# Causal row maxima in a four-block kernel: a fused masked reduction on VectorE against a split over three engines

## The chip, the cores and the metric

The kernel runs on one core of a Trainium2 chip. The metric is device time in microseconds (us), the median of several executions. Engines go by the profile's short names: PE (TensorE, matmuls and transposes), DVE (VectorE), ACT (ScalarE), POOL (GpSimd), SP (SyncE, which issues most DMAs). SBUF is the on-chip memory; PSUM is the small memory that matmuls write, eight banks of 512 fp32 numbers per partition.

## The reference, cut to what matters

Four blocks run one after the other on x of shape (2, 1024, 128), each followed by a layer norm: a retention block, then block 2 (causal attention with 16 heads of width 8, and four experts), then a block of attention over the full row, then a matmul with ternary weights. The change lies in the causal attention of the second block:

```python
scores = jnp.einsum('bhqd,bhkd->bhqk', q, k) / np.sqrt(HEAD_DIM)
causal = jnp.tril(jnp.ones((t, t), dtype=bool))
scores = jnp.where(causal, scores, -jnp.inf)
attn = jax.nn.softmax(scores, axis=-1)
out = jnp.einsum('bhqk,bhkd->bhqd', attn, v)
```

The softmax subtracts the largest score of each row, so each query needs the maximum over the keys that it may see.

## The kernel before, in words

**Stages.** The retention block fills the first 255 us or so. From there on, one hand-written schedule of 224 ticks (`chain_tick`, run from tick 3 on by the loop at L1102, ticks 0 to 2 by hand before it) does both attentions; the experts, projections and norms of the blocks are cut into pieces that `side_work` puts ahead of the ticks by due times. All of it is in manual order: each engine runs its instructions in the order in which the Python code issues them.

**Steps and items.** A step (L307) is one attention (a = 0 causal, a = 1 full), one sequence b, one block k of 512 queries, one group g of four heads. Its score items (`s_items`, L313 to L319) are tiles of 128 queries (number c) by up to 512 keys. In a causal step with k = 0 there are four, the **diagonal items**, c = 3, 2, 1, 0, with n = 512, 384, 256, 128 keys; the last 128 keys of each are the ones that the mask cuts. A causal step with k = 1 has four full items (512 keys of the first half) and after them its four diagonal items. So the causal attention has 96 items, ticks 0 to 95, of which 64 are diagonal; the full attention has ticks 96 to 223, eight items of 512 keys a step.

**A tick** does five things. `score` (L324) computes the item's scores by queries, one PSUM bank a head (tile `sc`). `maxima` (L338) reduces each to row maxima (`parts`): a diagonal tile by the fused `tensor_tensor_reduce` with the tile `causal` on DVE (L345; the profile shows a custom instruction and an accumulator read), another by `tensor_reduce` (L350). `shifted` (L373) computes the scores of the item 11 ticks back again, transposed, keys by queries (`sct`), now with the maxima subtracted, which enter as a row of `qT`; `exps` (L390) takes the exponential on ACT (L394), `bar` (L396) zeroes the masked corner on POOL (L402), and one tick later `product` (L408) multiplies with the values (tile `acc`), ACT copies the result out (L416, L419) and POOL adds it up (L420). Heads go in two halves: scores of heads 0 and 1 with transposed scores of 2 and 3, then the other way round. PE's order in a tick is thus sc0 sc1 sct2 sct3 sc2 sc3 sct0 sct1 acc, ACT's is e2 e3 e0 e1 (exponentials), then the copy of acc.

**From maxima to qT.** When a step's last item is through, `shifts` (L352) reduces `parts` to one number per query and head (tile `lowered`), `enter` (L362), one tick later, transposes it on PE (`m_ps`), ACT copies it (L370), and a DMA on SP's queue (L371) puts it into `qT`. The step's first transposed item is read 11 ticks after its first score item (AHEAD = 11).

**The ring.** All of these PSUM tiles, and those of the side work, take turns in a ring of eight banks (`ring_of`, L161). A tick takes nine, so `acc` takes the bank of the same tick's sc0 and cannot start before DVE is done with it; the next tick's tiles follow in the same way.

**Side work that the prediction names.** In ticks 3 and 4 `padding` for the second sequence (L230) fills tiles on POOL (L232 to L235) and `kT` on ACT (L236). In ticks 7 to 25 `mla_inputs` (L250) makes the second sequence's queries and keys; its rotary step works on POOL (L266, L269). From about tick 36 the experts take two tiles of the ring a tick: `ph` (L940, biased and rectified by ACT at L945 and DVE at L943) or `pmoe` (added up by DVE at L955).

## Time and profile before

| what | value |
|---|---|
| median of 4 runs (range) | 1208.35 us (1208.13 to 1210.31) |
| the profiled execution's own time | 1206.45 us |
| its span, first to last instruction | 1204.7 us |
| ticks 0 to about 17 (260 to 330 us) | PE 63.24 of 70.00 us busy, DVE 49.31, ACT 28.16, POOL 27.02 |
| the rest of the causal ticks (330 to 655 us) | PE 308.07 of 325.00 us busy, DVE 221.58, ACT 191.04, POOL 136.93 |
| most of the full attention (655 to 1150 us) | PE 469.77 of 495.00 us busy, DVE 385.19, ACT 343.27, POOL 173.62 |

An engine is busy while it runs an instruction. Matmul ends are modelled, so a busy PE need not be at its peak. A line such as "L345 DVE CUSTOM ... xN | busy, mean" is a group of like instructions; what follows the second bar is the engine's idle time ahead of them and what ended it. In the timeline a row gives start, length, engine, line, tiles and how many were merged, and in brackets the idle time ahead of it with the engine and tile that ended it.

### The profile page before, as it was taken

What the parts mean: (1) busy time and instruction counts of PE and PEld (TensorE: products, weight loads), DVE (VectorE), ACT (ScalarE), POOL (GpSimd) and SP (SyncE); (2) the same over time, 40 slices, a digit from 0 to 9 for tenths busy, and PEclk for the clock granted to TensorE, in tenths of its full rate; (3) what the DMA queues carried; (4) which work ended last, traced back from release to release, by engine and by line L of the source; (5) the groups of instructions that cost most, each with busy time, mean ns of one, the idle gap of its engine ahead of it and who ended that gap; (6) DMA issues with size and microseconds to landing.
All of it is one profiled execution on the core that took longest, in us unless ns stands there. A gap on an engine that the chain in (4) does not pass through costs nothing.

```text
span 1204.7 us, 22194 instructions
## 1 busy us (share of the span) xinstructions
PE 1111.5 (92%) x8554; PEld 607.3 (50%) x8554; DVE 830.9 (69%) x1822; ACT 711.0 (59%) x1439; POOL 478.1 (40%) x491
## 2 busy tenths in 40 slices
PE   6999999988899999999999999999989989998993
PEld 4888778755444555445544454444433333333321
DVE  3666677657667666676676667767788878888822
ACT  2455544432656645664565557555768877886892
POOL 3465544513645433452434334333233333333342
PEclk8999999965989999999999999999999999999996
DMA  8212121002000000010010001000100000000000
GB/s 263 66 45 54 36 45 41 23 11 78 19 10 10 1 1 2 4 20 1 1 19 2 1 3 19 2 1 1 19 10 2 2 2 10 1 2 10 2 1 9
DMA packets 14840, 25.56 MB, mean 21 GB/s; under 512 B 2960, under 2 KB 8400, under 8 KB 14352
## 3 DMA queue, kind: packets, MB, share of 16 engines
q1 hardware_dynamic: 14080, 22.30, 7.6%
q8 instruction: 67, 1.10, 0.4%
q0 software_dynamic: 224, 1.05, 0.2%
q10 hardware_dynamic: 432, 0.81, 0.2%
q14 instruction: 37, 0.30, 0.1%
HBM read 10.13 MB, written 1.05 MB: 9 GB/s over the span
## 4 chain that ended last, share of the span: by engine, by line
PE 73%; DVE 15%; POOL 5%; issue 3%; ACT 2%; DMA 1%; SPq 0%; POOLq 0%; DVEq 0%; ACTq 0%
PE sc L82 16%; PE acc L82 15%; PE sct L82 12%; PE pmoe L82 5%; PE ph L82 5%; DVE parts L350 4%; DVE spare L345 2%; PE pv L82 2%; PE py L82 2%; PE pr L82 2%; PE pg L82 1%; PE pout L707 1%; ACT es L394 1%; PE o_ps L186 1%; PE psc L82 1%
## 5 line engine op out<-in xcount | busy, mean ns | idle before, releaser
L394 ACT ACTIVATE es<-sct 128x512 f32<-128x512 f32 (+3 forms) x896 | 427.2, 559 | 213.5 <-PE sct L82 161.0
L350 DVE TENSOR_REDUCE parts<-sc 128x1 f32<-128x512 f32 x640 | 397.0, 682 | 94.7 <-PE sct L82 67.2
L82 PE MATMUL sc<-kT,qT 32*128 32x512 f32 (+3 forms) x1792 | 427.0, 587 | 0.9 <-DVE parts L345 0.9
L82 PE MATMUL sct<-qT,kT 32*128 32x512 f32 (+3 forms) x1792 | 411.7, 577 | 1.4 <-DMA qT<-m_rows 1.1
L420 POOL TENSOR_TENSOR oT<-oT,part 128x512 f32<-128x512 f32 (+3 forms) x192 | 217.1, 1131 | 398.9 <-ACT part L419 394.9
L82 PE MATMUL acc<-es,v_aug 128*32 128x512 f32 (+3 forms) x1792 | 222.8, 561 | 39.9 <-DVE parts L350 28.4
L82 PEld LDWEIGHTS sc<-kT,qT 32*128 32x128 f32 x1792 | 169.9, 190 | 141.0 <-DVE parts L350 74.2
L82 PEld LDWEIGHTS sct<-qT,kT 32*128 32x128 f32 x1792 | 179.2, 184 | 45.1 <-issue 22.4
L345 DVE CUSTOM_DVE_ANT_0 spare<-sc,causal 128x512 f32<-128x512 f32 (+3 forms) x256 | 125.5, 490 | 55.5 <-PE sc L82 21.3
L82 PEld LDWEIGHTS acc<-es,v_aug 128*32 128x32 f32 x1792 | 37.9, 108 | 197.1 <-DVE parts L350 112.5
L419 ACT COPY part<-acc 128x512 f32<-128x512 f32 (+3 forms) x192 | 105.8, 551 | 42.7 <-PE acc L82 34.5
L402 POOL TENSOR_SCALAR_AFFINE_SELECT es<-es 128x512 f32<-128x512 f32 x64 | 40.6, 634 | 101.6 <-ACT es L394 101.6
L764 ACT ACTIVATE og<-pt,cols_sb 128x128 f32<-128x128 f32 x128 | 46.4, 468 | 36.5 <-PE pt L756 36.5
L82 PEld LDWEIGHTS pmoe<-m_w,hT 128*128 128x128 f32 x512 | 59.6, 192 | 15.9 <-DVE parts L350 8.8
L82 PE MATMUL pmoe<-m_w,hT 128*128 128x128 f32 x512 | 65.0, 280 | 0.4
L82 PE MATMUL ph<-xnT,m_w 128*128 128x512 f32 x128 | 62.4, 610 | 0.0
L118 POOL TENSOR_TENSOR rstd<-rstd,nhalf 128x4 f32<-128x4 f32 (+1 forms) x44 | 54.6, 1242 | 3.6
L943 DVE TENSOR_SCALAR hT<-ph,cols_sb 128x512 f32<-128x512 f32 x32 | 24.0, 751 | 34.6 <-PE ph L82 34.6
L955 DVE SCALAR_TENSOR_TENSOR moe_acc<-pmoe,oh,moe_acc 128x128 f32<-128x128 f32 x64 | 22.4, 351 | 35.3 <-PE pmoe L82 34.9
L661 ACT COPY v<-pv 128x1024 f32<-128x1024 f32 x16 | 16.2, 1012 | 51.5 <-PE pv L82 51.5
L638 POOL TENSOR_TENSOR swap<-swap,r_cs 128x1024 f32<-128x1024 f32 x16 | 37.7, 2359 | 21.5 <-DMA swap<-plain 21.5
L82 PE MATMUL py<-r_wo,og 128*128 128x128 f32 x256 | 35.3, 296 | 6.2 <-DVE mrope L262 3.9
(177 smaller groups left out, 1200.0 us busy)
## 6 DMA issues: line engine op xcount, KB each, us to landing
swap<-plain SPq DMA_DIRECT2D x64, 128.0 KB
qT<-dense SPq DMA_DIRECT2D x32, 64.0 KB
kT<-dense SPq DMA_DIRECT2D x32, 64.0 KB
m_w<-in_m_w SPq DMA_DIRECT2D x2, 1024.0 KB
x<-in_x SPq DMA_DIRECT2D x4, 256.0 KB
mcs<-in_m_const SPq DMA_DIRECT2D x4, 256.0 KB
out<-ob SPq DMA_DIRECT2D x4, 256.0 KB
r_rest<-in_r_const POOLq DMA_DIRECT2D x1, 774.0 KB, 7.6
```

The source lines that it names most:

```text
L82: nc.tensor.matmul(o, lhsT, rhs, start=start, stop=stop)
L118: nc.gpsimd.tensor_tensor(r, r, nhalf[:, :n], ALU.pow)
L345: nc.vector.tensor_tensor_reduce(out=spare[:, :n], in0=sc[:, :n], in1=causal[:, BT - n :], scale=1.0, scalar=-3.0e38, op0=ALU.add, op1=ALU ...
L350: nc.vector.tensor_reduce(part, sc[:, :n], AX.X, ALU.max)
L394: nc.scalar.activation(es[n_item][:, j, :n], sct[:, :n], AF.Exp, scale=scale)
L402: nc.gpsimd.affine_select(out=d, in_=d, pattern=[[0, GH], [1, P]], compare_op=ALU.is_ge, fill=0.0, base=0, channel_multiplier=-1,)
L419: nc.scalar.copy(part[:, lo:], acc[:, lo:])
L420: nc.gpsimd.tensor_tensor(sums[i][:, lo:], sums[i][:, lo:], part[:, lo:], ALU.add)
L638: nc.gpsimd.tensor_tensor(swap[n], swap[n], table(n, 1), ALU.mult)
L764: nc.scalar.activation(og[:, a, g, :], pt[a][:, g, :], AF.Identity, bias=col("gn_b", h), scale=col("gn_w", h))
L943: nc.vector.tensor_scalar(hT[:, f, :], ph, bias, 0.0, ALU.add, ALU.max)
L955: nc.vector.scalar_tensor_tensor(acc[:, c, :], py[:, :P], oh[:, c, e : e + 1], acc[:, c, :], ALU.mult, ALU.add)
```

## The change

A diagonal tile is no longer reduced in one fused instruction. ACT copies its last 128 columns into one SBUF tile for all four heads (`corner`, two buffers); POOL overwrites the masked part there with -3e38 (`mask`, one `affine_select`); DVE takes the row maxima of all four heads at once from it (`barred`, one reduction, which stands one tick later between that tick's two halves), and, from PSUM, of the open columns ahead of the corner, n - 128 of them (none for c = 0). `parts` gets one more column; the open part of c = 0, which does not exist, is filled with -3e38 by POOL. In the steps with k = 1 the diagonal items now come first and the full items after them. In the steps with k = 0, whose last item is a diagonal one, `shifts` and `enter` come one tick later. The tile `causal` goes, with its set-up; the zeros that two DMAs took from it come from a small tile.

```diff
--- before.py
+++ after.py
@@ -3,7 +3,7 @@
 import concourse.bass as bass
 import concourse.tile as tile
 from concourse import mybir
-from concourse.masks import make_causal_mask, make_identity
+from concourse.masks import make_identity
 from concourse._compat import with_exitstack
 
 F32 = mybir.dt.float32
@@ -24,6 +24,7 @@
 NE, FF = 4, 512
 NF = FF // P
 NEG = -1.0e9
+LOWEST = -3.0e38
 NH = NG * GH
 VW = HD + 1
 VN = (NH - 1) * VW + HW
@@ -84,10 +85,8 @@
 
     ident = const.tile([P, P], F32, name="ident")
     make_identity(nc, ident)
-
-    causal = const.tile([P, BT], F32, name="causal")
-    nc.gpsimd.memset(causal, 0.0)
-    make_causal_mask(nc, causal[:, BT - P :], mask_val=-1.0e30)
+    zeros = const.tile([GH, P], F32, name="zeros")
+    nc.gpsimd.memset(zeros, 0.0)
     nhalf = const.tile([P, 16], F32, name="nhalf")
     nc.gpsimd.memset(nhalf, -0.5)
     ones = const.tile([P, P], F32, name="ones")
@@ -308,17 +307,21 @@
         (a, b, k, g) for a in range(2) for b in range(B) for k in range(NB) for g in range(NG)
     ]
 
+
     s_items, t_items = [], []
     for i, (a, b, k, g) in enumerate(steps):
         if a == 0:
+            s_items += [(i, c, k, (c + 1) * P) for c in reversed(range(NC))]
             s_items += [(i, c, half, BT) for half in range(k) for c in range(NC)]
-            s_items += [(i, c, k, (c + 1) * P) for c in reversed(range(NC))]
             t_items += [(i, kt, max(0, kt * P - k * BT)) for kt in range((k + 1) * NC)]
         else:
             s_items += [(i, c, half, BT) for half in range(NB) for c in range(NC)]
             t_items += [(i, kt, 0) for kt in range(T // P)]
     s_last = {it[0]: n for n, it in enumerate(s_items)}
+
+    s_done = {i: n + (steps[i][0] == 0 and steps[i][2] == 0) for i, n in s_last.items()}
     t_last = {it[0]: n for n, it in enumerate(t_items)}
+    corners = {}
     parts, lowered, es, sums, pools, o_tok = {}, {}, {}, {}, {}, []
 
     def score(item, heads):
@@ -326,7 +329,9 @@
         a, b, k, g = steps[i]
         tok = slice(k * BT + c * P, k * BT + (c + 1) * P)
         if i not in parts:
-            parts[i] = small.tile([P, NC, GH, NB], F32, tag="parts", name="parts")
+            parts[i] = small.tile([P, NC, GH, NB + 1], F32, tag="parts", name="parts")
+            if a == 0:
+                nc.gpsimd.memset(parts[i][:, 0, :, k : k + 1], LOWEST)
         got = []
         for j in heads:
             sc = slot("sc")
@@ -335,24 +340,46 @@
             got.append((j, sc))
         return got
 
-    def maxima(item, got):
+    def diagonal(item):
+
         i, c, half, n = item
         a, b, k, g = steps[i]
-        for j, sc in got:
-            part = parts[i][:, c, j, half : half + 1]
-            if a == 0 and half == k:
-                spare = early.tile([P, BT], F32, tag="spare", name="spare")
-                nc.vector.tensor_tensor_reduce(
-                    out=spare[:, :n], in0=sc[:, :n], in1=causal[:, BT - n :], scale=1.0,
-                    scalar=-3.0e38, op0=ALU.add, op1=ALU.max, accum_out=part,
+        return a == 0 and half == k
+
+    def maxima(item, got):
+
+        i, c, half, n = item
+        open_n = n
+        if diagonal(item):
+            open_n = n - P
+            if item not in corners:
+                corners[item] = small.tile([P, GH, P], F32, tag="corner", name="corner", bufs=2)
+            for j, sc in got:
+                nc.scalar.copy(corners[item][:, j, :], sc[:, open_n:n])
+        if open_n:
+            for j, sc in got:
+                nc.vector.tensor_reduce(
+                    parts[i][:, c, j, half : half + 1], sc[:, :open_n], AX.X, ALU.max
                 )
-            else:
-                nc.vector.tensor_reduce(part, sc[:, :n], AX.X, ALU.max)
+
+    def mask(item):
+
+        d = corners[item]
+        nc.gpsimd.affine_select(
+            out=d, in_=d, pattern=[[0, GH], [-1, P]], compare_op=ALU.is_ge, fill=LOWEST,
+            base=0, channel_multiplier=1,
+        )
+
+    def barred(item):
+        i, c, half, n = item
+        nc.vector.tensor_reduce(
+            parts[i][:, c, :, half + 1], corners.pop(item), AX.X, ALU.max
+        )
 
     def shifts(i):
 
         a, b, k, g = steps[i]
-        n_half = NB if a else k + 1
+        n_half = NB if a else k + 2
         lowered[i] = small.tile([P, GH, NC], F32, tag="lowered", name="lowered")
         nc.vector.tensor_reduce(
             lowered[i].rearrange("p j c -> p c j"), parts[i][:, :, :, :n_half], AX.X, ALU.max,
@@ -450,6 +477,8 @@
     def starts(a, b, k):
         return s_first[step_of(a, b, k, 0)]
 
+    done_at = {n: i for i, n in s_done.items()}
+
     def chain_tick(tick):
         si = tick if tick < n_items else None
         ti = tick - AHEAD if 0 <= tick - AHEAD < n_items else None
@@ -458,18 +487,21 @@
             got_t = shifted(ti, t_heads) if ti is not None else ()
             if si is not None:
                 maxima(s_items[si], got_s)
+                if s_heads[0] == 0 and 0 < si and diagonal(s_items[si - 1]):
+                    barred(s_items[si - 1])
             if ti is not None:
                 exps(ti, got_t)
         if ti is not None:
             bar(ti)
-        if si is not None and s_last[s_items[si][0]] == si:
-            shifts(s_items[si][0])
+        if si is not None and diagonal(s_items[si]):
+            mask(s_items[si])
+        if tick in done_at:
+            shifts(done_at[tick])
         ai = tick - AHEAD - 1
         if 0 <= ai < n_items:
             product(ai)
-        si = tick - 1
-        if 0 <= si < n_items and s_last[s_items[si][0]] == si:
-            enter(s_items[si][0])
+        if tick - 1 in done_at:
+            enter(done_at[tick - 1])
         ai = tick - AHEAD - 3
         if 0 <= ai < n_items and t_last[t_items[ai][0]] == ai:
             finish(t_items[ai][0])
@@ -1006,7 +1038,7 @@
             for g in range(NG):
                 nc.sync.dma_start(
                     out=qT[b][ONE::HW, g, :],
-                    in_=causal[:GH, :P].unsqueeze(1).to_broadcast([GH, T // P, P]),
+                    in_=zeros.unsqueeze(1).to_broadcast([GH, T // P, P]),
                 )
         tp = transposed(x2[b][k], "x2_ps")
         x2T = scratch("joT", "x2T", (P, BT))
```

## The prediction, on record before the changed kernel ran

> **What bounds the kernel now.** The page first: PE is the busiest engine, and the chain of waits that ended last is mostly PE. The fused maxima (spare, L345) hold 2% of the chain's span, other maxima (L350) 4%.

> ```profile
> span 1204.7 us, 22194 instructions
> PE 1111.5 (92%) x8554; PEld 607.3 (50%) x8554; DVE 830.9 (69%) x1822; ACT 711.0 (59%) x1439; POOL 478.1 (40%) x491
> ...
> PE 73%; DVE 15%; POOL 5%; issue 3%; ACT 2%; DMA 1%; SPq 0%; POOLq 0%; DVEq 0%; ACTq 0%
> ```

> So 2% of 1204.7, 24 us, is all that faster masked maxima could take directly. The windows by stage bound PE's idle time in the causal ticks at (70.00 - 63.24) + (325.00 - 308.07) = 24 us. Then the timeline, for what a tick waits for. Ticks with expert work (heavy, 4.5 to 5.3 us) differ from those without (light, 2.0 to 3.3 us). A heavy one with a full item, DVE and PE:

> ```profile
> 557.98 2.48 DVE L350 TENSOR_REDUCE parts<-sc 128x1 f32<-128x512 f32 x4 [0.30 <-PE sc L82]
> ```
> ```profile
> 556.82 0.70 PE L82 MATMUL sc<-kT,qT 32*128 32x512 f32 x2
> ...
> 558.82 0.64 PE L82 MATMUL acc<-es,v_aug 128*32 128x256 f32 x8 [0.60 <-DVE parts L350]
> ```

> The tick starts at 556.82; sc0 is ready 1.16 us later; its reduction lasts 0.68; acc starts 0.16 after that, having stood still for 0.60. The chain sc0, maximum, acc sets this tick's first part (2.00 us), since the transposed tiles are small. In a light step (487 to 498 us) DVE is the bound: fused reductions follow each other without a gap, at 0.84 us (512 columns), 0.71 (384), 0.57 (256) and 0.44 (128):

> ```profile
> 488.18 0.69 DVE L345 CUSTOM_DVE_ANT_0 spare<-sc,causal 128x512 f32<-128x512 f32 x1 [1.37 <-PE sc L82]
> ...
> 488.79 0.08 DVE L345 DVE_READ_ACCUMULATOR2_ANT parts<- 128x1 f32 x1
> 489.02 0.69 DVE L345 CUSTOM_DVE_ANT_0 spare<-sc,causal 128x512 f32<-128x512 f32 x1
> ```

> That is 4 x (0.84 + 0.71 + 0.57 + 0.44) = 10.24 us of the step's 11.0 (487.02 to 498.0).

> **Part 1: DVE's work.** Plain reductions: 0.682 us at 512 columns (L350), 0.276 at 128 (L986); by a straight line 0.41 at 256, 0.55 at 384. Four of 512 take 2.48 together, so the next starts 0.60 after the last, 0.08 less than one lasts. Per step: open parts 4 x (0.47 + 0.33 + 0.20) = 4.0; four corner reductions of 128x512 like L220 (0.679; 0.60 apart) 2.4; sum 6.4, or 7.7 if nothing overlaps. DVE saves 2.5 to 3.8 us a step, 40 to 61 us over 16 steps, worth something only where DVE is late.

> **Part 2: ACT's copies.** 256 of 128 columns. One lasts 0.291 (L419, 128x128), but four exponentials of 128 columns take 0.79, that is 0.17 apart:

> ```profile
> 558.12 0.79 ACT L394 ACTIVATE es<-sct 128x128 f32<-128x128 f32 x4 [1.37 <-PE sc L82]
> ```

> So 44 to 74 us. A light step has exponentials (2.15 + 1.64 + 1.2 + 0.9 = 5.9), copies of acc (0.62 + 0.48 + 0.37 + 0.27 = 1.7), m_rows 0.25: 7.9 us of 11.0. With 16 x 0.17 it is 10.6, with 16 x 0.29 12.5. I take 0.17, the row of the same engine, shape and direction; the other end is a rival.

> **Part 3: an order between ACT and DVE.** In the changed program every reduction of an open part waits for ACT's copy of the same bank, not for PE. So the chain becomes sc0, copy, maximum, acc: 0.29 for the copy and a handover. No handover from ACT to DVE stands alone in the trace; it lies between 0 and the 0.16 of DVE to PE; I take 0.10. The second pair is copied only after two exponentials.

> [...]

> Heavy ticks, start to acc, from the timeline (score columns, transposed columns): (512,384) 2.00 with a gap of 0.21, (512,256) 1.99 with 0.39, (512,128) 2.00 with 0.60, (512,512) 1.93 to 1.99, (384,512) 1.97, (256,512) 1.96, (128,512) 1.57, (384,256) 1.66, (256,128) 1.35. After: with sc0 ready at 1.16, 0.90 and 0.72 us, plus 0.29 + 0.10, the reduction (0.55, 0.41, 0.28) and 0.16, acc starts at 2.26, 1.86, 1.55 in the three diagonal ticks; the fourth has no reduction on DVE from PSUM, 1.57.

> **Part 4: the new order (k = 1).** The diagonal items now meet the small transposed tiles, the full items the large ones. Leading four ticks before: 2.00 + 1.99 + 2.00 + 1.99 = 7.98; after 2.26 + 1.86 + 1.55 + 1.57 = 7.24: -0.74. Trailing four before: 1.93 + 1.97 + 1.96 + 1.57 = 7.43; after 4 x 1.95 = 7.8: +0.4.

> **Part 5: POOL.** 64 masks at 0.634 (L402, same extent), 41 us, and 16 small fills (0.33 each by L233). POOL is 42% busy here, so its time is covered; if not, the mask is late, and DVE, which waits for it in the middle of the next tick, holds the reductions of heads 2 and 3 and so the ring. In a light tick the mask ends some 0.6 to 0.9 us ahead of that point (exponentials end at +3.6, two selects, 4.9; DVE is there at about +5.5). Behind the rotary pair (2.36 + 1.27 us, four times in ticks 11 to 25) it is late. Between 0 and 4 x 3.6 us; I take +1.0, because the causal zeroing (L402), which acc needs, waits behind the same pair already.

> **Part 6: the rest, at nothing.** shifts and enter a tick later in eight k = 0 steps: six ticks are left until qT is read, over 12 us, against 4.98 of the longest m_rows landing on the chain; SP's order stays as it is. The set-up of causal goes at the start, under the loads. Ticks 3 and 4: copies stand behind four fills of kT (4.27 us), a mask behind four fills of qT (3.91); DVE comes out level there, then gains.

> **The sum** (a step's eight ticks have a leading and a trailing half):
> - heavy leading halves, 3 (ticks 40, 72, 80): 3 x -0.74 = -2.2
> - heavy trailing halves, 5 (36, 44, 68, 76, 92): +2.0
> - heavy k = 0 step, 1 (48): 0.25 + 0.2 + 0.2 = +0.65
> - light k = 0 steps, 4 (12, 52, 56, 60): DVE no longer the bound; PE's own sum there is score parts 1.79 + 1.66 + 1.35 + 1.57 = 6.4, acc 1.06 + 0.85 + 0.64 + 0.43 = 3.0, transposes 0.9: 10.3; with ACT at 10.6 I take 10.6 for 11.0: -1.6
> - light leading halves, 5 (16, 24, 32, 64, 88): -0.3 each by the same relief: -1.5
> - light trailing halves, 3 (20, 28, 84): +0.2 each: +0.6
> - ticks 0 to 11, where DVE works almost without a gap: three steps save 2.5 or more each, some 7.5, but most of it is lost again behind the fills and at the side work's own chain; between -7.5 and +1 (copies that wait out the fills), I take -1.5
> - POOL +1.0

> Together -2.6 us. The profiled execution took 1206.45: 1203.85. The median lies 1.90 above that execution: 1205.8.

> **Rivals.**
> 1. *ACT becomes the bound* (slower). If a copy costs its whole 0.29, light steps take 12.5 instead of 10.6. Nine light halves or steps hold diagonal items (4 + 5): 9 x 1.9 = 17; if side work hides half, 8.5. On the -2.6 that is +6 to +14; 1216, nearer the lower end, since most of the nine have some side work. It decides from a copy spacing of (11.0 - 7.9)/16 = 0.19 us, little above my 0.17: that speaks for it; against it, L394's row.
> 2. *The mask comes late* (slower): POOL behind side work, four rotary pairs and the experts' bias additions; 4 x 1.5 us = +6, and with the -2.6 about 1212. It decides once a mask ends more than the 0.6 to 0.9 us of Part 5 late.
> 3. *DVE's relief is worth more*: the fused maxima's 24 us on the chain shrink by 2.5/10.24 to 3.8/10.24: -6 to -9; 1200.
> 4. *Nothing is gained*: PE holds the causal ticks at 95% after 330 us, and the two halves of Part 4 cancel: 1208.

> **The numbers.** About 0.2%, 2.4 us, is what a measurement of this kernel can tell from no change. The forecast's own band is -6 to +1, with 0.45, of which 0.27 lies beyond -2.4 and 0.18 within; rival 3 has 0.13, rival 4 0.07, rival 1 0.23, rival 2 0.12. So faster 0.40, same 0.25, slower 0.35. The range, 1198 to 1218, leaves out the far ends of rivals 1 and 3.

> **What would show it.** Right: acc's gaps behind DVE smaller at 40 to 42 and 72 to 74, light steps near 10.6 us with PE or ACT without gaps, ACT copies 0.17 apart. Wrong: PE or DVE waiting for corner copies or for POOL's corner selects by more than a few us in the list of waits; a causal stage longer than 395 us (260 to 655). If the full attention's ticks (655 to 1150) changed by more than 1 us, my picture of the change is wrong.

## The result, and the profile after

| | before | after |
|---|---|---|
| median of all executions, us (range) | 1207.54 (1202.59 to 1211.99, 77 runs) | 1209.35 (1203.19 to 1215.00, 54 runs) |
| ratio after/before | | 1.0016, 95% interval 1.0008 to 1.0024 |
| the profiled execution: own time, span, us | 1206.45, 1204.7 | 1213.78, 1212.0 |
| its mean granted clock of PE | 0.964 | 0.955 |

The changed kernel is slower, by 1.8 us. The forecast was 1205.8 us, 2.6 below before; 1209.35 lies inside its range of 1198 to 1218, but on the other side of no change. Two profiles alone do not show why, because each is one draw of the granted clock, and the changed kernel's was a low one. So both kernels were profiled once more, and the tables below use those too.

From the page of the changed kernel: the engines, the chain, and the groups that replaced the fused maxima.

```profile
span 1212.0 us, 22176 instructions
...
PE 1114.3 (92%) x8554; PEld 608.0 (50%) x8554; DVE 809.2 (67%) x1566; ACT 750.3 (62%) x1695; POOL 516.7 (43%) x569
...
PE 73%; DVE 14%; POOL 5%; ACT 3%; issue 3%; DMA 1%; SPq 0%; POOLq 0%; DVEq 0%; ACTq 0%
...
L361 DVE TENSOR_REDUCE parts<-sc 128x1 f32<-128x512 f32 (+3 forms) x832 | 469.2, 620 | 143.7 <-PE sct L83 80.5
...
L358 ACT COPY corner<-sc 128x128 f32<-128x128 f32 x256 | 56.7, 292 | 44.4 <-PE sc L83 35.1
...
L368 POOL TENSOR_SCALAR_AFFINE_SELECT corner<-corner 128x512 f32<-128x512 f32 x64 | 40.6, 635 | 39.8 <-ACT corner L358 36.2
L375 DVE TENSOR_REDUCE parts<-corner 128x4 f32<-128x512 f32 x64 | 43.5, 680 | 19.4 <-POOL corner L368 16.1
```

DVE's work fell by 21.7 us (830.9 to 809.2). ACT got 39.3 and POOL 38.6 more. PE, the busiest engine, has the same 8554 matmuls. DVE's share of the chain fell from 15% to 14%, ACT's rose from 2% to 3%. L375 shows the new dependence: of its 19.4 us of idle time 16.1 ended with POOL's mask.

The list of waits of the changed kernel, causal ticks (total us, times, longest), gives the prices of the new order among engines:

```profile
DVE parts L361 <- ACT corner L358: 49.9, 41, 5.6
...
DVE parts L375 <- POOL corner L368: 16.1, 12, 3.6
...
PEld acc L83 <- POOL es L429: 11.0, 10, 2.2
...
PE acc L83 <- POOL es L429: 5.9, 6, 1.8
```

The first is long but is not what loses: e3 below keeps it, at 54.0 us, and is 5.7 us faster. The last is PE itself standing still for POOL's zeroing of `es`, a step that the change did not touch. The same list of before has it too, only 0.9 us shorter in all, so what counts is where it falls:

```profile
PE acc L82 <- POOL es L402: 5.0, 5, 1.8
```

**Where the time went.** Lengths of groups of four ticks in us, from the start of the first score matmul of each. "r_" are the second profiles; the clock is that of the profiled execution.

| ticks | before (.964) | r_before (.971) | after (.955) | r_after (.959) | what they are |
|---|---|---|---|---|---|
| 0 to 11 | 42.65 | 41.07 | 40.46 | 41.88 | light k = 0 |
| 12 to 23 | 49.05 | 47.00 | 49.22 | 47.87 | light, then the first k = 1 step |
| 24 to 27 | 16.24 | 15.04 | 16.00 | 14.82 | light leading half |
| 28 to 31 | 15.23 | 15.23 | 16.76 | 15.47 | light trailing half |
| 32 to 35 | 12.93 | 12.92 | 16.09 | 16.08 | light leading half |
| 36 to 39 | 20.60 | 20.60 | 22.62 | 21.97 | heavy trailing half |
| 40 to 43 | 18.65 | 18.64 | 17.51 | 17.51 | heavy leading half |
| 44 to 47 | 19.59 | 19.59 | 19.96 | 19.96 | heavy trailing half |
| 48 to 63 | 59.58 | 59.59 | 58.35 | 58.35 | k = 0 steps, one heavy, three light |
| 64 to 71 | 32.04 | 32.03 | 33.71 | 33.03 | first k = 1 step of the second sequence |
| 72 to 95 | 109.87 | 109.88 | 110.44 | 110.45 | the other k = 1 steps |
| 96 to 222 | 491.31 | 491.35 | 491.31 | 491.29 | full attention |

Where a row differs between both profiles of a kernel, a clock draw is in it; where it agrees, it is the work's, or both drew alike. The gains are there (40 to 43, 48 to 63), and the full attention is unchanged, as the prediction had required. The largest loss stands in ticks 32 to 39: 3.2 us and 1.4 to 2.0 us, in both profiles. But in both of them half clock began inside ticks 32 to 35 (at 397.2 and 394.0 us) and lasted 10.2 us, so these two rows alone do not part the work from the clock. The table starts at tick 0, which itself starts 2 to 4 us later in the profiles of after (263.3 and 263.8 us, against 260.3 and 261.2). That is no cost of the change: in e1, e7 and e8 below, which have the set-up of before, it starts at 264.8 to 265.1.

The same spot in the two timelines. Before, POOL (the product xn of the experts' norm, then the zeroing) and PE's acc:

```profile
390.00 1.04 POOL L223 TENSOR_TENSOR xn<-xa,rstd 128x512 f32<-128x512 f32 x1
391.00 0.63 POOL L402 TENSOR_SCALAR_AFFINE_SELECT es<-es 128x512 f32<-128x512 f32 x1
```
```profile
391.68 0.64 PE L82 MATMUL acc<-es,v_aug 128*32 128x256 f32 x8 [0.22 <-POOL es L402]
```

After:

```profile
389.32 0.64 POOL L429 TENSOR_SCALAR_AFFINE_SELECT es<-es 128x512 f32<-128x512 f32 x1 [0.19 <-ACT es L421]
389.91 0.63 POOL L368 TENSOR_SCALAR_AFFINE_SELECT corner<-corner 128x512 f32<-128x512 f32 x1
390.51 1.28 POOL L447 TENSOR_TENSOR oT<-oT,part 128x512 f32<-128x512 f32 x1
391.87 0.19 POOL L116 TENSOR_SCALAR rstd<-ss 128x4 f32<-128x4 f32 x1
392.15 1.02 POOL L117 TENSOR_TENSOR rstd<-rstd,nhalf 128x4 f32<-128x4 f32 x1
393.25 1.04 POOL L222 TENSOR_TENSOR xn<-xa,rstd 128x512 f32<-128x512 f32 x1
394.24 0.63 POOL L429 TENSOR_SCALAR_AFFINE_SELECT es<-es 128x512 f32<-128x512 f32 x1
```
```profile
394.93 0.64 PE L83 MATMUL acc<-es,v_aug 128*32 128x256 f32 x8 [1.79 <-POOL es L429]
```

Only the first row has idle time ahead of it; behind it POOL has no break. Before, POOL was already level with PE here: acc waited 0.22 us for it. After, a mask of 0.63 us stands in the queue, PE is ready for acc earlier against POOL's queue, and the stand (idle time of PE before an instruction) is 1.79 us. What follows is read from the windows of the changed kernel; the figure behind POOL's count is the granted clock:

```profile
390.00:398.00 8.00, 6.01 (x60) 3.70 (x55) 3.94 (x11) 5.22 (x22) 7.75 (x11) 0.95 0.01 2
398.00:406.00 8.00, 8.00 (x44) 3.74 (x41) 3.39 (x11) 3.83 (x10) 2.60 (x4) 0.50 0.01 2
```

PE, the first column after the length, is idle for 2 of the first 8 us, with POOL busy for 7.75 of them. Then PE is busy throughout at half clock. Before, the same ticks ran at full clock.

### The profile page after: what moved, and what is told of

Same layout as the page of the kernel before. It is cut to its first block, busy times and chain, and to the rows that moved or that the text cites. A ratio compares the mean times of both kernels' runs of the same rounds, so it can differ in the third digit from the quotient of the medians.

```text
span 1212.0 us, 22176 instructions
## 1 busy us (share of the span) xinstructions
PE 1114.3 (92%) x8554; PEld 608.0 (50%) x8554; DVE 809.2 (67%) x1566; ACT 750.3 (62%) x1695; POOL 516.7 (43%) x569
## 3 DMA queue, kind: packets, MB, share of 16 engines
HBM read 10.13 MB, written 1.05 MB: 9 GB/s over the span
## 4 chain that ended last, share of the span: by engine, by line
PE 73%; DVE 14%; POOL 5%; ACT 3%; issue 3%; DMA 1%; SPq 0%; POOLq 0%; DVEq 0%; ACTq 0%
PE sc L83 16%; PE acc L83 15%; PE sct L83 12%; DVE parts L361 5%; PE pmoe L83 5%; PE ph L83 5%; PE pv L83 2%; PE py L83 2%; PE pr L83 2%; ACT es L421 2%; PE pg L83 1%; PE pout L739 1%; PE o_ps L185 1%; PE psc L83 1%; DVE x L203 1%
## 5 line engine op out<-in xcount | busy, mean ns | idle before, releaser
L361 DVE TENSOR_REDUCE parts<-sc 128x1 f32<-128x512 f32 (+3 forms) x832 | 469.2, 620 | 143.7 <-PE sct L83 80.5
L421 ACT ACTIVATE es<-sct 128x512 f32<-128x512 f32 (+3 forms) x896 | 435.2, 569 | 167.9 <-PE sct L83 145.2
L83 PE MATMUL sct<-qT,kT 32*128 32x512 f32 (+3 forms) x1792 | 422.8, 589 | 2.1 <-DMA qT<-m_rows 1.9
L83 PEld LDWEIGHTS sct<-qT,kT 32*128 32x128 f32 x1792 | 183.5, 187 | 49.8 <-issue 26.8
L358 ACT COPY corner<-sc 128x128 f32<-128x128 f32 x256 | 56.7, 292 | 44.4 <-PE sc L83 35.1
L368 POOL TENSOR_SCALAR_AFFINE_SELECT corner<-corner 128x512 f32<-128x512 f32 x64 | 40.6, 635 | 39.8 <-ACT corner L358 36.2
L375 DVE TENSOR_REDUCE parts<-corner 128x4 f32<-128x512 f32 x64 | 43.5, 680 | 19.4 <-POOL corner L368 16.1
```

The lines of the kernel that those rows point to most:

```text
L83: nc.tensor.matmul(o, lhsT, rhs, start=start, stop=stop)
L358: nc.scalar.copy(corners[item][:, j, :], sc[:, open_n:n])
L361: nc.vector.tensor_reduce(parts[i][:, c, j, half : half + 1], sc[:, :open_n], AX.X, ALU.max)
L368: nc.gpsimd.affine_select(out=d, in_=d, pattern=[[0, GH], [-1, P]], compare_op=ALU.is_ge, fill=LOWEST, base=0, channel_multiplier=1,)
L375: nc.vector.tensor_reduce(parts[i][:, c, :, half + 1], corners.pop(item), AX.X, ALU.max)
L421: nc.scalar.activation(es[n_item][:, j, :n], sct[:, :n], AF.Exp, scale=scale)
```

## The experiments

The theory after the result: the new order of the items is a gain; the split gives it back, and of the split it is the masks on POOL. Rivals: the order is what loses; ACT's copies are what loses; the loss is a draw of the clock alone. Each kernel had 4 to 12 executions, beside executions of before on the same chip. The ratio is to before, with its 95% interval.

**r_before, r_after: both kernels unchanged.**

> The kernel before, unchanged, to read each run's granted clock beside its time. Theory 'gate' (the runs of one kernel differ, and the two kernels differ, by how long TensorE's clock was granted at half; the waits that the change moves sum to about the -3 us forecast): the times of this kernel fall on one line over the granted clock, as those of the changed kernel do (0.955: 1213.5, 0.968: 1203.4, some 0.7 us for each thousandth), and at the same clock it is 0 to 3 us slower than the changed one. Theory 'masks' (late masks behind GpSimd hold VectorE and so TensorE, in ticks 27 to 36 and 91, by more than the rest gains): at the same clock it is about 2 us faster than the changed one.

1208.37 us, ratio 0.9994 (0.9979 to 1.0010).

> The changed kernel once more, unchanged, for a second profile and more executions on this chip. If the time follows the granted clock (about -0.75 us for each +0.001), this profile lies on the line through 1213.5 at .955 and 1203.4 at .968 within 1.5 us, and the ticks 32 to 36 and 24 to 28 tell whether their losses are there at another draw of the clock too: 16 us each if the work sets them, 13 and 15 if the clock did.

1209.72 us, ratio 1.0021 (1.0003 to 1.0039); its profiled execution took 1210.54 at 0.959, 0.2 us from the line. Ticks 32 to 35 lasted 16.08 again, but with half clock in 6.0 us of them, as in 4.7 us of them in the first profile; e3 and e6 below part the two. Ticks 24 to 27 lasted 14.82: what the first profile had lost there was the clock.

**e1_order_only: before, with the diagonal items leading.**

```diff
         if a == 0:
+            s_items += [(i, c, k, (c + 1) * P) for c in reversed(range(NC))]
             s_items += [(i, c, half, BT) for half in range(k) for c in range(NC)]
-            s_items += [(i, c, k, (c + 1) * P) for c in reversed(range(NC))]
```

> The fused masked reduction as before, only the diagonal items of the k = 1 steps ahead of the full ones. By the table of ticks: heavy leading halves 3 x -1.4 us (no copy in the chain), trailing halves 5 x +0.4, and some 2 us more where the full items of a sequence's first k = 1 step meet the small transposed tiles of the k = 0 steps: about -0.5 us, 1207. If it is the order that lets the clock fall (small scores beside small transposed tiles), it is as slow as the whole change or slower, 1209 to 1211, at a lower clock than before. 'Masks' expects no loss: 1207.

1205.28 us, ratio 0.9978 (0.9962 to 0.9994). The order alone is faster. Its heavy leading halves take 17.08 us, 0.43 less than in the changed kernel.

**e2_split_only: the changed kernel with the items in the old order.** The corner reduction of the last item then falls into the next step, so in all causal steps the shifts come a tick later.

```diff
-            s_items += [(i, c, k, (c + 1) * P) for c in reversed(range(NC))]
             s_items += [(i, c, half, BT) for half in range(k) for c in range(NC)]
+            s_items += [(i, c, k, (c + 1) * P) for c in reversed(range(NC))]
...
-    s_done = {i: n + (steps[i][0] == 0 and steps[i][2] == 0) for i, n in s_last.items()}
+    s_done = {i: n + (steps[i][0] == 0) for i, n in s_last.items()}
```

> The split reduction with the diagonal items at the end of a step as before (shifts and enter one tick later in all causal steps). By the table: diagonal ticks beside 512-column transposed tiles, +0.3 us in the first of each heavy half (5 of them), light k = 0 steps gain 0.5 each: about 0, 1207 to 1208, plus up to 3 us where the row of maxima now lands two ticks ahead of its use. 'Masks' expects the loss here, 1210 or more; 'order lets the clock fall' expects 1207 and the clock of before.

1214.01 us, ratio 1.0052 (1.0031 to 1.0073). The split alone is a loss; ticks 24 to 27 last 22.37 us in its profile. In these ticks PE waits 3.81 us for the DMA of `m_rows`, and half clock begins. The later shifts are part of this kernel, so it is no pure price of the split.

**e7_order_by_step: before, with the diagonal items leading except in the first k = 1 step of each sequence.**

```diff
-            s_items += [(i, c, half, BT) for half in range(k) for c in range(NC)]
-            s_items += [(i, c, k, (c + 1) * P) for c in reversed(range(NC))]
+            full = [(i, c, half, BT) for half in range(k) for c in range(NC)]
+            own = [(i, c, k, (c + 1) * P) for c in reversed(range(NC))]
+            s_items += own + full if g else full + own
```

> The fused reduction as before; diagonal items lead in the k = 1 steps except the first of each sequence, where the full items would meet the small transposed tiles of the k = 0 steps (ticks 68 to 71 took 1.7 us more with diagonals leading everywhere; ticks 16 to 23 were even). If the order works by pairing large with large: 1 to 2 us faster than the order-only kernel, 1203.5 to 1204.5. If its gain had another source, such as the clock: the same as order-only, 1205.3, or slower.

1203.70 us, ratio 0.9969 (0.9953 to 0.9985). Ticks 68 to 71 are back at 18.49 us (20.15 in e1), and 16 to 19 at 15.11 (16.04). In those ticks the transposed tiles belong to the last k = 0 step, small ones at the end, so the new order pairs large with large first and full items with small ones last. By the medians 1.6 us better than e1, within the intervals of both.

**e3_no_mask: the changed kernel without the masks.**

```diff
-        if si is not None and diagonal(s_items[si]):
-            mask(s_items[si])
```

> The changed kernel without GpSimd's masks: the corner's maxima are taken over masked scores too, which leaves out the causal rule in the maxima alone. 64 x 0.635 us leave GpSimd, and VectorE's corner reduction waits for ScalarE alone. 'Masks': the stalls behind GpSimd go, 3 to 5 us faster than the changed kernel, 1205. 'Gate': 0 to 2 us faster, and the time still goes with the clock.

1203.64 us, ratio 0.9965 (0.9945 to 0.9986): 5.7 us less than the changed kernel. ACT's 256 copies and the corner reductions are all still there. So the copies are not what loses; the masks are. Ticks 32 to 35 last 12.97 us at full clock, and acc's stand is shorter by 0.59 us, nearly the length of one mask (0.63 us):

```profile
391.29 0.64 PE L83 MATMUL acc<-es,v_aug 128*32 128x256 f32 x8 [1.20 <-POOL es L429]
```

The rest of the stand's growth from 0.22 us is there without any mask.

**e10_mask_aside: the masks are made as before, but into a tile that nobody reads.** This keeps POOL's work and takes away DVE's wait for it.

```diff
+        aside_ = small.tile([P, GH, P], F32, tag="aside", name="aside", bufs=2)
         nc.gpsimd.affine_select(
-            out=d, in_=d, pattern=[[0, GH], [-1, P]], compare_op=ALU.is_ge, fill=LOWEST,
+            out=aside_, in_=d, pattern=[[0, GH], [-1, P]], compare_op=ALU.is_ge, fill=LOWEST,
```

> The changed kernel with GpSimd's masks still made, from the same copies and at the same place in its order, but written to a tile that nobody reads; VectorE reduces the unmasked corner and waits for ScalarE alone. It leaves the causal rule out of the maxima. 'GpSimd's time' (64 more selects delay its zeroing, its sums and its norms, which TensorE and ScalarE need): as slow as the changed kernel, 1208 to 1210. 'The extra hop' (the corner's maxima come late because they wait for GpSimd): as fast as the kernel without masks, 1203 to 1205.

1204.49 us, ratio 0.9984 (0.9962 to 1.0005), but in two groups: eight executions at 1202.9 to 1204.9 with a clock of 0.966 or more, four at 1210.4 to 1211.9 with 0.959. The profiled one is of the second group: the same stand of 1.79 us before acc at 392.32, ticks 32 to 35 16.09 us long, half clock behind it. So the longer stand comes from POOL's occupied time, not from DVE's wait for the mask. Whether the first group had the stand without the half clock can't be seen, because no profile fell into it. As a comparison of medians this run is inconclusive. At equal clock (last section) it comes to 1206.5 us, nearer to the changed kernel's 1207.1 than to the 1204.5 of e3, which speaks for POOL's time.

**e5_mask_ahead: the mask ahead of the zeroing in POOL's order.**

```diff
-        if ti is not None:
-            bar(ti)
         if si is not None and diagonal(s_items[si]):
             mask(s_items[si])
+        if ti is not None:
+            bar(ti)
```

> The changed kernel with the corner's mask ahead of the causal zeroing of the exponentials in GpSimd's order. Its input, the copies, is there about 1 us before the last exponential, so the mask runs in GpSimd's idle time. 'Masks': 2 to 5 us faster than the changed kernel, 1204 to 1207, at a higher mean clock (0.963 or more against 0.961); the stall of acc behind GpSimd near 395 us stays, since GpSimd is busy with the norm there. 'Copy in the chain': no change, within 1 us.

1209.07 us, ratio 1.0014 (0.9994 to 1.0034): a miss, nothing gained. DVE gets its mask earlier and acc its zeroing later; the stand in ticks 32 to 35 is 2.12 us.

**e6_corner_late: the corner reduction after all four reductions of the next tick.**

```diff
-                if s_heads[0] == 0 and 0 < si and diagonal(s_items[si - 1]):
+                if s_heads[0] == 2 and 0 < si and diagonal(s_items[si - 1]):
```

> The changed kernel with the corner's reduction after all four open reductions of the next tick instead of between its halves, so that a late mask holds nothing but what follows the tick's maxima. 'Masks, by way of VectorE' (VectorE waits for the mask in the middle of a tick): 2 to 4 us faster than the changed kernel. 'Masks, by way of GpSimd' (the masks delay GpSimd's zeroing of the exponentials and its norms, which TensorE needs): within 1 us of the changed kernel.

1209.80 us, ratio 1.0020 (1.0004 to 1.0036). No gain: DVE's wait for the mask is not what costs, and the stand is 2.00 us here. In this profile no half clock followed it, and ticks 32 to 35 last 14.09 us: by that, some 2 us of the 16.08 above are the half clock's.

**e4_dve_first: DVE's reductions ahead of ACT's copies.** The statement that makes the copies moves behind the reductions:

```diff
-            for j, sc in got:
-                nc.scalar.copy(corners[item][:, j, :], sc[:, open_n:n])
         if open_n:
...
+        if open_n < n:
+            for j, sc in got:
+                nc.scalar.copy(corners[item][:, j, :], sc[:, open_n:n])
```

> The changed kernel with the two readers of a score bank in the other order: VectorE's open reduction first, then ScalarE's copy, which now waits for it. 'Masks' (GpSimd's masks come late, and TensorE's waits and half-clock windows in ticks 24 to 36 follow): copies, and so exponentials and masks, come later still, 1 to 4 us slower than the changed kernel, 1210 to 1213, at a clock no higher. 'Copy in the chain' (the copy ahead of VectorE is the cost): the open maxima come 0.3 us earlier, the changed kernel minus 1 to 3 us.

1228.53 us, ratio 1.0173 (1.0148 to 1.0198): far worse than expected. Its waits:

```profile
ACT corner L364 <- DVE parts L359: 73.2, 80, 4.7
...
DVE parts L376 <- POOL corner L369: 37.8, 30, 3.6
```

The copies wait for DVE, and the exponentials stand behind them in ACT's queue; ticks 56 to 59 last 14.28 us in place of 10.13. Here a wait cost by what queues behind it: the same two reads of one bank, in the other order, cost 19 us (1228.53 against 1209.35).

**e14_split_outside and e15_split_inside: the loss placed.** Both have the order of the changed kernel. Ticks 12 to 39 are four steps: the last k = 0 step of the first sequence and its first three k = 1 steps. e14 splits everywhere but there, e15 only there; the rest keeps the fused maxima.

```diff
+    def split(i):
+        a, b, k, g = steps[i]
+        return a == 0 and i not in (3, 4, 5, 6)     # e15: i in (3, 4, 5, 6)
...
+        if a == 0 and half == k and not split(i):
+            for j, sc in got:
+                spare = early.tile([P, BT], F32, tag="spare", name="spare")
+                nc.vector.tensor_tensor_reduce(
```

> As the changed kernel in its order (diagonal items lead in all steps with k = 1), but the four steps that fill ticks 12 to 39 (second k = 0 step of the first sequence's later groups and its first k = 1 steps) keep the fused maxima, without copies and masks; the split is made in the other twelve causal steps. Theory A (the split loses in ticks 12 to 39, where POOL has the rotary pairs and norms of the side work to do and a mask or a zeroing is late): most of the 4 us between the changed kernel (1209.35) and the order alone (1205.28) goes: 1204 to 1206, with ticks 24 to 28 below 15 us and ticks 32 to 36 near 12.7. Theory B (the split's cost lies in all causal ticks alike, by busier ACT and POOL): only 4/16 of it goes: 1208 to 1209. By the granted clock: under A the mean clock is near .965, under B near .962.

1204.49 us, ratio 0.9975 (0.9958 to 0.9993).

> The counterpart: the same order, the split only in the four steps that fill ticks 12 to 39, fused maxima in the other twelve. Theory A (the loss is in these ticks): 1208 to 1210, as the changed kernel, with ticks 32 to 36 near 16 us. Theory B (spread over all steps): 1205.3 + 4/16 of 4 = 1206 to 1207.

1210.94 us, ratio 1.0021 (0.9999 to 1.0043). Twelve of the sixteen steps can be split and the kernel stays as fast as with the order alone; the other four bring the whole loss. Ticks 32 to 35 last 13.07 us in e14 and 16.10 in e15. In e14 the POOL rows of this place have no mask, the zeroing is done when PE arrives, and acc does not wait:

```profile
386.64 1.04 POOL L223 TENSOR_TENSOR xn<-xa,rstd 128x512 f32<-128x512 f32 x1
387.63 0.64 POOL L445 TENSOR_SCALAR_AFFINE_SELECT es<-es 128x512 f32<-128x512 f32 x1
```
```profile
388.50 0.64 PE L83 MATMUL acc<-es,v_aug 128*32 128x256 f32 x8
```

Its windows stay at a clock of 1.00:

```profile
382.00:390.00 8.00, 7.62 (x66) 3.35 (x59) 6.34 (x22) 4.86 (x15) 7.56 (x11) 1.00 0.01 2
390.00:398.00 8.00, 6.99 (x59) 3.47 (x54) 5.75 (x20) 5.33 (x11) 2.20 (x3) 1.00 0.01 2
```

**e16_norm_moved and its control e17_order_norm_moved: 1.04 us of other work taken from POOL's queue just there.** In the first expert block's norm:

```diff
+        if moved:
+            yield 1
         xn = scratch(lane + "xn", "xn")
-        nc.gpsimd.tensor_tensor(xn, src, r.unsqueeze(2).to_broadcast([P, NC, P]), ALU.mult)
-        yield 2
+        engine = nc.vector if moved else nc.gpsimd
+        engine.tensor_tensor(xn, src, r.unsqueeze(2).to_broadcast([P, NC, P]), ALU.mult)
+        yield 1 if moved else 2
```

> The changed kernel with its copies and masks as they are; of the first expert block's norm, which falls into ticks 32 to 35, the one product xn (1.04 us on POOL in the changed kernel's trace) is made by DVE and one tick later. If the loss comes from POOL's queue there (a mask of 0.63 us a tick ahead of the zeroing that acc waits for), the stand of 1.79 us before acc becomes 0.8 or less, ticks 32 to 36 take 13 to 14.5 us in place of 16.1, and if such a stand is also what brings the half clock behind it, ticks 36 to 40 take 21 us in place of 22 to 22.6 and the median is 1204.5 to 1206.5, the mean clock near .965. If the stand and the clock have nothing to do with each other: the stand goes but the half clock stays, 1208 to 1209. If the loss is not POOL's: 1209.5.

1207.82 us, ratio 0.9998 (0.9984 to 1.0013).

> The control: the order alone with fused maxima (1205.28), and the same product moved from POOL to DVE. There is no mask on POOL and no long stand before acc in these ticks, so by the theory of POOL's queue nothing is gained: 1205 to 1206, ticks 32 to 36 near 12.7 us. If the product's move is worth something by itself, it is below 1204, and the gain of the other kernel would not speak for the masks.

1205.38 us, ratio 0.9978 (0.9966 to 0.9990), as without the move. So the move is worth something only where there are masks, some 1.5 us by the medians, less than expected and with intervals that overlap a little, and all of it by the clock: e16's mean clock is 0.9641, the changed kernel's 0.9613, and at equal clock e16 is no faster. In e16's profile ticks 32 to 35 last 13.44 us and 36 to 39 21.24, as expected, at full clock. But the stand shrank only to 1.52 us and changed its cause, DVE in place of POOL:

```profile
391.79 1.11 DVE L225 TENSOR_TENSOR xn<-xa,rstd 128x512 f32<-128x512 f32 x1 [0.82 <-POOL rstd L117]
```
```profile
393.25 0.64 PE L83 MATMUL acc<-es,v_aug 128*32 128x256 f32 x8 [1.52 <-DVE parts L364]
```

DVE now waits 0.82 us for POOL's rstd, takes 1.11 for xn, and its maxima, which free acc's bank, are late instead. The wait was moved, not removed. The other ticks that e15 loses in (28 to 31 at 16.75, half clock again) are as in the changed kernel.

**e8_plain, e9_plain_by_step, e13_split_light: what DVE's relief is worth.** e8 is before with plain reductions for all items, e9 the same with e7's order, e13 is e7 with the split in three light steps only (ticks 52 to 63).

```diff
-            if a == 0 and half == k:
-                spare = early.tile([P, BT], F32, tag="spare", name="spare")
-                nc.vector.tensor_tensor_reduce(
...
-            else:
-                nc.vector.tensor_reduce(part, sc[:, :n], AX.X, ALU.max)
+            nc.vector.tensor_reduce(part, sc[:, :n], AX.X, ALU.max)
```

> The kernel before, with plain reductions over all n columns of the diagonal tiles instead of fused ones: no masks, no copies, and the causal rule left out of the maxima. It shows what any unfused form could gain at most in the old order: VectorE's 10.24 us a step become some 7.5. Light k = 0 steps gain 0.5 to 1.0 us each, the heavy ones little, since TensorE holds them; 1203 to 1206. If it is as fast as before, 1208, VectorE's work there bounded nothing.

1199.28 us, ratio 0.9929 (0.9907 to 0.9951).

> Both at once: plain reductions over all n columns (the causal rule left out of the maxima) and the diagonal items first except in a sequence's first k = 1 step. If order and reduction act in different ticks, their gains add: some 4.5 us by the order, 2 to 4 by the reduction, 1200 to 1202. If both remove the same waits, 1203.

1194.36 us, ratio 0.9886 (0.9861 to 0.9911).

```diff
+    def split(i):
+        a, b, k, g = steps[i]
+        return a == 0 and b == 1 and k == 0 and g > 0
```

> The order by step with fused reductions, and the split with copies and masks only in the three k = 0 steps of the second sequence after its first, ticks 52 to 63, where the changed kernel gained 0.6, 0.9 and 0.2 us. Expected 1.5 us faster than order-by-step, 1202 to 1203; the clock as there, since GpSimd has little else to do in these ticks. 'GpSimd's time' and 'the extra hop' expect the same here.

1204.43 us, ratio 0.9965 (0.9949 to 0.9982): no better than e7. Relief that costs no other engine anything is worth 9 us by e9 against e7; relief by a split over three engines gave none back even in light steps, although ticks 56 to 59 take 10.13 us with it, 11.02 before and 9.64 in e8. The fastest kernel is e9, at 1194.4; of those that keep the causal rule in the maxima it is e7, at 1203.7. Both beat before and the changed kernel.

## Why the prediction was wrong, point by point

**What held.** Part 1: the reductions last 0.68, 0.55, 0.42 and 0.28 us, the corner reductions 0.68, as taken. Part 2: two copies take 0.43 to 0.47 us, so their spacing is 0.14 to 0.18 by the length of 0.29 of one; rival 1, which needed 0.19 or more, is out. Part 4's sign: the order gains in the leading halves and loses in the trailing ones. Part 6: in the causal ticks no matmul waits for the m_rows of a k = 0 step; the one wait for m_rows, in tick 91 for a k = 1 step, is 1.85 us (before 1.12). POOL's extra work did not slow DVE's own instructions here: a reduction of 512 columns lasts 0.682 us before and 0.681 after, by the means of 640. Light k = 0 steps: ticks 52 to 63 give 0.59, 0.89 and 0.19, together 1.7 us against 1.2 forecast for these three.

**The signs of being wrong.** Two of those that the prediction named came true: DVE waits 49.9 us for corner copies and 16.1 us for POOL's masks, and ticks 0 to 95 take 401.1 and 397.4 us in place of 396.4 and 391.6. The first sign was a poor one, since e3 keeps the wait for the copies, and e10 takes away the wait for the masks without taking away PE's stand.

**Part 3, the handover: sized too high.** In the changed kernel's heavy tick 40 (start 424.48) the copy of sc0 starts 1.16 us after the start, as forecast:

```profile
425.64 0.43 ACT L358 COPY corner<-sc 128x128 f32<-128x128 f32 x2 [2.28 <-PE sc L83]
```
```profile
425.94 2.13 DVE L361 TENSOR_REDUCE parts<-sc 128x1 f32<-128x384 f32 x4 [1.00 <-ACT corner L358]
```
```profile
426.64 1.06 PE L83 MATMUL acc<-es,v_aug 128*32 128x512 f32 x8 [0.37 <-DVE parts L361]
```

The reduction starts 0.30 after the copy, which lasts 0.29: a handover of 0.01, where I took 0.10. acc starts 2.16 after the start of the tick (forecast 2.26).

**The sum, term by term.** "Measured" is r_after minus r_before; where a row was drawn at half clock, e16, which has the same work there, is named. Differences of single profiles, in us.

| term | forecast | measured |
|---|---|---|
| heavy leading halves (40, 72, 80) | -2.2 | -1.13, -1.12, -1.13: -3.4 |
| heavy trailing halves (36, 44, 68, 76, 92) | +2.0 | +0.64 (e16), +0.37, +1.21, +0.37, +0.25 (e16): +2.8 |
| heavy k = 0 step (48) | +0.65 | +0.43 |
| light k = 0 steps (12, 52, 56, 60) | -1.6 | +0.32, -0.59, -0.89, -0.19: -1.35 |
| light leading halves (16, 24, 32, 64, 88) | -1.5 | +0.89, -0.22, +3.16, -0.21, +1.21: +4.8 |
| light trailing halves (20, 28, 84) | +0.6 | -0.34, +0.24, +0.30: +0.2 |
| ticks 0 to 11 | -1.5 | +0.8 |
| POOL | +1.0 | in the light halves above |
| together | -2.6 | +4.3 |

The measured column is that of profiles granted 0.959 and 0.971, so half clock is still in it where e16 does not stand in (above all in 32, 88 and 0 to 15).

Two terms failed.

*The light leading halves.* I gave all five the same relief. Three of them lose. In 16 it is the order: e1, without copies or masks, takes 16.04 us there, against 15.11 in r_before; e7, which leaves the first step of each sequence alone, has 15.11. In 88 it is a draw of the clock, at least for the most part: with the same order e1 takes 15.08 and e17 13.91, against 13.86. In 32 it is POOL and the half clock: PE's stand there grows by 1.57 us, and about 2 us of the 3.16 are the half clock's, since e6, with a stand of 2.00 us at full clock, takes 14.09. The first step of a sequence is also the +1.21 at 68 (e7: no loss). I had taken every k = 1 step's transposed neighbours to be those of a k = 1 step.

*Part 5, POOL, the step that turned the sign.* It said that the mask is late only behind the rotary pair of ticks 11 to 25, and took "+1.0, because the causal zeroing (L402), which acc needs, waits behind the same pair already". At the rotary pairs the reason held: acc's waits for the zeroing behind three of them are 0.39, 0.41 and 1.32 us after, 1.08, 0.76 and 1.78 before, and 0.41 and 1.33 at the last two in e3, without masks. But the place that loses is another, the norm in ticks 32 to 35. There a zeroing that already waits is no cover but the opposite: its queue is full, and of a further 0.63 us 0.59 go to PE. The profile of before showed it: POOL without a break from 383.84 to 393.87, and acc with 0.22 us of waiting for it. I had read POOL's average, 42% busy, as cover. e15 against e1 prices ticks 12 to 39: four split steps cost 5.7 us, of which 2.2 are left at equal clock. e14 against e1 shows the other twelve cost nothing (-0.8 us, within the intervals).

**What had no term at all: the granted clock.** At equal clock the changed kernel is the faster one (last section): about 1207.1 against 1208.9 us at 0.964, -1.8 where -2.6 was forecast. But its mean clock over all executions is 0.9613, before's 0.9655; 0.0042 times 780 us is 3.3 us the other way. The sum of both, +1.5, is the measured +1.8 within its interval. The theory that stands: the masks lengthen POOL's queue where it is already full (a stand of 1.79 us in place of 0.22), PE stands still, and in four of the profiles, named below, half clock follows. The direct wait is the smaller part: of the 5.7 us that e3 gains by leaving the masks out, 2.6 are left at equal clock. That the stand is what brings the half clock is supported, not proved. In ticks 32 to 39 no profile whose longest stand in ticks 32 to 35 is 1.2 us or less has half clock; all four with the 1.79 us stand (after, r_after, e10, e15) have some 10 us of it; e4 (1.23 us) has 13.7, e5 (2.12 us) one short stretch, and e6 (2.00 us), e16 (1.52 us) and e9 (1.32 us) none. Counted over all 19 profiles, between 300 and 660 us, half clock began during a stand of 1.5 us or more, or within 3.4 us of its end (the length of the shortest stretch in the last section), in 30 of 35 cases; for stands of 1.0 to 1.5 us in 10 of 54. Of the 53 stretches of half clock there, 13 began without a stand of 1 us near them. So half clock was frequent at a long stand here, was not forced by one, and also began without one. An experiment that stops PE for a set time, with nothing else changed, was not made.

**The rivals.** Rival 2, the late mask (1212), is the one that came true in kind, with another price and through the zeroing rather than through DVE: e6 and e10 take away or move DVE's wait, and PE's stand stays. Rival 3's relief exists (e8, e9), but is not to be had with this split. Rival 4, nothing gained, was nearest in size, 1208, by luck: its two halves nearly cancel (-3.4 and +2.8), but the order alone is a gain (e1), and its reasons name neither POOL nor the clock.

## What to carry to other kernels

Before moving work to an engine that is idle on average, look in the timeline for the places where it runs without a break and where the bounding engine already waits for it, even for 0.2 us: there an added instruction can go to the end at nearly full price (0.59 of 0.63 us here), and a few such ticks can take back what the rest of the change brings. Price an order of items by what each item is paired with at every boundary, not by the middle of the run. And where the executions of one kernel differ in the granted clock (0.955 to 0.968 for the changed kernel here), compare kernels by many executions and by that clock, since a single pair of profiles here differed by 7 us where the medians differ by 1.8.

## What the runs showed of the hardware

**The time followed the granted clock of the draw.** Over all executions here whose clock is on record but one (of before, 3518.37 us at a clock of 1.0), with one offset a kernel, a mean clock higher by 0.001 goes with a time shorter by 0.78 us, and what is left scatters by about 1.2 us. The offsets, at a clock of 0.964, are estimates: one slope stands for half clock in all stages.

| kernel | median us | mean clock | us at 0.964 |
|---|---|---|---|
| before | 1207.5 to 1208.7 | 0.9655 | 1208.9 |
| after | 1209.35 | 0.9613 | 1207.1 |
| e1, order | 1205.28 | 0.9631 | 1204.7 |
| e3, no mask | 1203.64 | 0.9657 | 1204.5 |
| e15, split inside | 1210.94 | 0.9601 | 1206.9 |
| e14, split outside | 1204.49 | 0.9648 | 1205.1 |
| e10, mask aside | 1204.49 | 0.9642 | 1206.5 |
| e7, order by step | 1203.70 | 0.9637 | 1203.8 |
| e9, plain by step | 1194.36 | 0.9658 | 1195.7 |

e14 and e15 differ by 6.5 us in the medians, and by 1.8 at equal clock.

```profile
332.30:335.70 3.40, 3.40 (x24) 2.44 (x20) 1.77 (x4) 1.47 (x5) 2.90 (x5) 0.50 0.02 5
366.40:373.30 6.90, 6.90 (x38) 2.47 (x38) 2.87 (x5) 4.35 (x12) 2.52 (x5) 0.51 0.14 21
397.20:407.40 10.20, 10.20 (x51) 4.51 (x45) 4.80 (x12) 5.36 (x14) 3.40 (x5) 0.50 0.01 2
```

PE is busy throughout in all three. Which stretches a kernel got differed from one execution to the next, with the same instructions: ticks 24 to 27 of the changed kernel took 16.00 us in one profile and 14.82 in the other.

PE's idle time between matmuls in the causal ticks of this profile was 2.03 us at most. From 300 to 660 us of it four stands last over 1 us: 1.38 us (its end at 331.83), 1.32 (348.74), 1.79 (394.93) and 1.85 (640.12); half clock began within 2.5 us after the first and the third (at 332.3 and 397.2), during the fourth (at 639.5), and not after the second. Three further stretches (from 308.4, 366.4 and 533.7) began with no such stand near them. So in this profile no length of a stand parts the stretches: three of the six began without a stand over 1 us, and 1.38 us was followed by half clock where 1.32 us was not.

**A fused masked reduction took longer than a plain one.** On tiles of the same size it started every 0.84 us at 512 columns, a plain one every 0.60. e8, whose 64 diagonal items have plain reductions, shows what that is worth on the whole: 1 - 0.9929 of 1208 us, 8.6 us.
